# A written-out order of issue gets a list of its own for its beginning: first-layer weights first, first group in pieces

## The chip, the core and the metric

The kernel runs on one core of one Trainium2 chip. Its engines are TensorE (PE; its weight loads are listed as PEld), VectorE (DVE), ScalarE (ACT), GpSimd (POOL) and SyncE (SP), which here only issues DMAs. Each engine works through its own instructions in program order, and waits for another engine or for a DMA at a semaphore. The metric is the device time of one execution in microseconds; three runs of the kernel before gave 1090.84, 1091.98 and 1093.44, with a median of 1091.98.

## The reference

There are 128 graphs of 128 nodes with 64 features, and two layers, each followed by a residual sum and a layer norm. The first layer has a hidden width of 192; the second is a gated recurrent update.

```python
mask = (adj > 0.0)
xj_proj = x @ W1a                                  # W1 = [W1a; W1b]
diff = x[:, :, None, :] - x[:, None, :, :]
h = relu(xj_proj[:, :, None, :] + diff @ W1b + b1) # b, j, k, 192
hm = einsum('bjkh,bjk->bjh', h, mask)
x = layernorm(x + hm @ W2 + deg[..., None] * b2)
# second layer, on the new x
m = relu(relu(x @ V1 + c1) @ V2 + c2)
msg = relu(adj @ m)
gi, gh = msg @ W_ih.T + b_ih, x @ W_hh.T + b_hh    # three gates of 64 each
r, z = sigmoid(i_r + h_r), sigmoid(i_z + h_z)
n = tanh(i_n + r * h_n)
x = layernorm(x + (1 - z) * n + z * x)
```

The sum over a node's neighbours in `hm` is nearly all of the work.

## The kernel before

**Tiling.** The 128 graphs go in 32 groups of four (`G = 4`). For a group the kernel loads the adjacency `adjT` (256 KB), `xT` (two transfers of 64 KB) and `x` (128 KB) in `load`. POOL makes the mask (`masks`, L390). A matmul and a DVE multiply give each neighbour its rank (`ranks`, `pc` and `rankT`), others the degrees (`degrees`, `pd`, `deg` and `larger`); from these come the overflow segments (`counts`, `offsets` with `past` and `own`, `places`). The DVE compares ranks with constants to make one-hot selections (`pick0` in eight steps, `pick1` in four, L498). The projections of the nodes are `values` (`pu`, two fp32 products and two of a bias in bf16, L508 and L511; ACT copies them to `uv`, L515), and `pieces` splits them into three bf16 parts (`b0`, `b1`, `b2`), with ACT, DVE, ACT and POOL taking turns; for the first group this goes graph by graph.

**The main work of a group** is 24 rounds, six for each of its four graphs. In a round ACT copies a row into a PSUM tile of two banks (`seed`, L561), PE adds the selected neighbours to it with twelve matmuls (`gather`, L592), and the DVE sums absolute values over it (`reduce`, L608). There are three such PSUM tiles, so at most three rounds are in flight. Of a graph's six rounds, four take `pick0` and are seeded from `uv`; two take `pick1` and are seeded from `us`, which is made in `over` (`pz`, L572). `owners` turns `own` (`pq`, `ownT`). Two more PSUM tiles of one bank, `ps_w`, serve all other products in turn: the product that is two further down the order waits until the tile has been read. The sums are put together on POOL (`together`), `second` ends the first layer, and `message1` to `update` are the second layer.

**What sets the order.** A planner does not run on the chip; the order is written out. Every part is a generator that stops at its `yield`s. `TIMETABLE` gives for each part the due time of each of its steps in a group; a group's times are shifted by `PER = 768` per group. All steps of all groups are sorted by due time and emitted in that order, and the instructions of a step are queued on their engines in that order. The times have no other meaning. For group 0 the list `FIRST` replaces the times of the parts that it names, and `SETUP` gives the times of the five steps of `setup`, which makes the constants and loads the weights.

**The beginning as it is emitted.** First come the transfers of group 0, then all of `setup`'s first block: SP issues two transfers of the first layer's weights (`wab`), `w2c`, `b1c`, and five rows that are spread over all 128 partitions (`b2bc`, `bias` from `b1`, `bi` from `b_ih`, `bias` from `b_hh` and from `g_b2`; L148). The first layer's folded weights (`wall`, `wT`, `cps`, `dps`) follow, and then one block that folds the bias rows and splits all 576 columns of `bias` into three bf16 rows in `three` (L202 to L219, eight DVE operations). The first 256 columns of `three` serve the first layer's `values`; the other 320 serve `message2` and `gates`. Then group 0's `values`, `pieces`, `pick0`, `offsets` and `places` come. A last step of `setup`, at -3000, clears `gw1` and `gw2` on the DVE (L223) and issues twelve transfers of the second layer's weights (L225 to L231). Only behind these comes the load of group 1 (at 768 - 1520 = -752), then `masks` of group 1 (-3), the load of group 2 (16), `degrees` and `ranks` of group 1 (208 to 315), `over` and `owners` of group 0 and, from 476 on, group 0's rounds: `seed`, `gather`, `reduce`.

Of the kernel before, what the change touches and what calls it, by code (L numbers as in the profile page):

```python
# [8 lines left out]
F32 = mybir.dt.float32  # L9
# [3 lines left out]
ALU = mybir.AluOpType  # L13
AX = mybir.AxisListType

N = 128
F = 64
H = 192
HC = 96
G = 4  # L20
K = 64
V = H + F
W0 = 8
W1 = 4
# [23 lines left out]
}  # L48


SETUP = (-4990, -4988, -4987, -4981, -3000)
FIRST = {
    "load": (-5000,), "masks": (-4989,), "ranks": (-4986, -4985), "degrees": (-4984, -4983), "counts": (-4982,),
    "offsets": (-4980, -4979, -4966, -4965, -4964, -4963, -4962), "turned": (-4978, -4977),
    "values0": (-4976, -4975, -4974), "values1": (-4971, -4970, -4969), "pieces": (-4972, -4968, -4959, -4958),
    "places": (-4961, -4960), "pick0": (-4973, -4973, -4967, -4967, -4957, -4957, -4956, -4956),
}


# [18 lines left out]
def adj_resnorm_kernel(  # L78
# [19 lines left out]
    nc = tc.nc  # L98
    NB = x.shape[1]
    ng = NB // G  # L100
    const = ctx.enter_context(tc.tile_pool(name="const", bufs=1))


    ident = const.tile([N, N], F32, name="ident")
    ident_h = const.tile([N, N], BF16, name="ident_h")
    upper = const.tile([N, N], F32, name="upper")
# [3 lines left out]
    strict = const.tile([N, N], BF16, name="strict")  # L110
    strict_w = const.tile([N, N], BF16, name="strict_w")
# [3 lines left out]
    zeros = const.tile([N, 512], BF16, name="zeros")  # L115
    nhalf = const.tile([N, G], F32, name="nhalf")
    nseg_all = const.tile([N, NB], BF16, name="nseg_all")
    iota = const.tile([N, N], BF16, name="iota")

    wab = const.tile([N, 2, H], F32, name="wab")  # L120
    wall = const.tile([N, 4 * N], F32, name="wall")
    w2c = const.tile([HC, 2, F], F32, name="w2c")
    b1c = const.tile([HC, 2], F32, name="b1c")
    b2bc = const.tile([N, F], F32, name="b2bc")
# [3 lines left out]
    NBI = V + 256 + F  # L128
    bias = const.tile([N, NBI], F32, name="bias")
    three = const.tile([N, NBI], BF16, name="three")  # L130
    bi = const.tile([N, H], F32, name="bi")
# [10 lines left out]
    def each(t, n):  # L142

        return t.rearrange("p (o c) -> p o c", o=1).to_broadcast([t.shape[0], n, t.shape[1]])

    def setup(ps_g, ps_w):
        def spread(t, src):
            nc.sync.dma_start(t, src.rearrange("(o n) -> o n", o=1).to_broadcast(list(t.shape)))  # L148

        for h in range(2):  # L150
            nc.sync.dma_start(wab[h * F : (h + 1) * F], w1.rearrange("(c f) h -> f c h", c=2))
        nc.sync.dma_start(w2c, w2.rearrange("(c h) f -> h c f", c=2))
        nc.sync.dma_start(b1c, b1.rearrange("(c h) -> h c", c=2))
        spread(b2bc, b2)
        spread(bias[:, 0:H], b1)
        spread(bi, b_ih)
        spread(bias[:, V + F : V + 256], b_hh)
        spread(bias[:, V + 256 : NBI], g_b2)
        make_identity(nc, ident)
        make_upper_triangular(nc, upper)  # L160
        nc.gpsimd.memset(nhalf, -0.5)
        nc.vector.memset(ones_h, 1.0)
        nc.vector.memset(halves, 0.0)
        for h in range(2):
            nc.vector.memset(halves[h * K : (h + 1) * K, h : h + 1], 1.0)
        nc.vector.memset(zeros, 0.0)
        nc.vector.tensor_copy(incl2, upper)
        nc.vector.memset(incl2[0:K, K:N], 0.0)
        nc.vector.tensor_copy(ident_h, ident)
        nc.vector.tensor_copy(incl, upper)  # L170
        nc.vector.tensor_sub(strict, upper, ident)
        nc.vector.tensor_scalar_mul(strict_w, strict, -float(W1))

        for i in range(3):
            p = ps_g.tile([N, 2, 512], F32, tag="g", name="pv")
            for c in range(2):
                nc.tensor.matmul(p[:, c, :], ones_h, zeros, start=True, stop=True)
        ips = ps_w.tile([N, N], F32, tag="w", name="ips")
        nc.tensor.matmul(ips, ones_h, strict, start=True, stop=True)
        yield  # L180
        nc.vector.tensor_copy(iota, ips)
        nc.vector.tensor_add(wall[:, 0:H], wab[:, 0, :], wab[:, 1, :])
        nc.vector.tensor_scalar_mul(wall[:, V : V + H], wab[:, 1, :], -1.0)
        nc.vector.tensor_scalar_mul(w2c, w2c, 0.5)
        yield

        tps = ps_w.tile([HC, 4, F], F32, tag="w", name="tps")
        for c in range(4):
            at = (V, V + HC, 0, HC)[c]
            nc.tensor.transpose(tps[:, c, :], wall[0:F, at : at + HC], ident[0:F, 0:F])  # L190
        nc.vector.tensor_copy(wT, tps.rearrange("p c (o f) -> p c o f", o=1).to_broadcast([HC, 4, 2, F]))
        yield
        cps = ps_w.tile([N, F], F32, tag="w", name="cps")
        for c in range(2):
            nc.tensor.matmul(cps, b1c[:, c : c + 1].to_broadcast([HC, N]), w2c[:, c, :], start=c == 0, stop=c == 1)
        dps = ps_w.tile([N, 2, F], F32, tag="w", name="dps")
        for d in range(2):
            for c in range(2):
                nc.tensor.matmul(dps[:, d, :], wT[:, 2 * d + c], w2c[:, c, :], start=c == 0, stop=c == 1)
        nc.vector.tensor_copy(wall[:, H:V], dps[:, 0, :])  # L200
        nc.vector.tensor_copy(wall[:, V + H : 4 * N], dps[:, 1, :])
        nc.vector.tensor_add(bias[:, H:V], cps, b2bc)  # L202
        nc.vector.tensor_copy(bias[:, V : V + F], bi[:, 128:H])
        nc.vector.tensor_add(bias[:, V + F : V + H], bias[:, V + F : V + H], bi[:, 0:128])

        nc.vector.tensor_scalar_mul(bias[:, V + 256 : NBI], bias[:, V + 256 : NBI], 0.5)
        at = const.tile([N, 3], F32, name="at")
        nc.vector.tensor_add(at, ident[:, 0:3], ident[:, F : F + 3])
        piece = const.tile([N, NBI], BF16, name="piece")
        for c in range(3):  # L210
            nc.vector.tensor_copy(piece, bias)
            if c == 0:
                nc.vector.tensor_scalar(three, piece, at[:, c : c + 1], None, ALU.mult)
            else:
                nc.vector.scalar_tensor_tensor(
                    out=three, in0=piece, scalar=at[:, c : c + 1], in1=three, op0=ALU.mult, op1=ALU.add
                )
            if c < 2:
                nc.vector.tensor_sub(bias, bias, piece)  # L219
        yield  # L220

        for t, src in ((gw1, g_w1), (gw2, g_w2)):
            nc.vector.memset(t, 0.0)  # L223
            for h in range(2):
                nc.sync.dma_start(t[h * F : (h + 1) * F, h * F : (h + 1) * F], src)  # L225
        for h in range(2):
            hs = slice(h * F, (h + 1) * F)
            nc.sync.dma_start(gb1[hs], g_b1.rearrange("(h o) -> h o", o=1))
            nc.sync.dma_start(wm[hs, 0:F], w_ihT[:, 128:H])
            nc.sync.dma_start(wm[hs, F:H], w_ihT[:, 0:128])  # L230
            nc.sync.dma_start(wx[hs, :], w_hhT)  # L231

    def wide(t, n, w=F):
        return t.rearrange("p (g o) -> p g o", o=1).to_broadcast([N, n, w])
# [130 lines left out]
    with ExitStack() as fast:  # L365
# [4 lines left out]
        ps_g = fast.enter_context(tc.tile_pool(name="ps_g", bufs=3, space=bass.MemoryType.PSUM))  # L370
        ps_w = fast.enter_context(tc.tile_pool(name="ps_w", bufs=2, space=bass.MemoryType.PSUM))

        def load(s):
            g = s["g"]
            gs = slice(g * G, (g + 1) * G)
            s["adjT"] = loads.tile([N, G, N], F32, tag="adjT", name=f"adjT{g}")
            nc.sync.dma_start(s["adjT"], adjT[:, gs, :])

            s["xT"] = loads.tile([N, 2, N], F32, tag="xT", name=f"xT{g}")
            for h in range(2):  # L380
                nc.sync.dma_start(s["xT"][h * F : (h + 1) * F], xT[:, g * G + 2 * h : g * G + 2 * h + 2, :])
            s["x"] = loads.tile([N, G, F], F32, tag="x", name=f"x{g}")
            nc.sync.dma_start(s["x"], x[:, gs, :])

        def prep_parts(s):
            g = s["g"]
# [287 lines left out]
        def storer(g):  # L674
            return lambda o: nc.sync.dma_start(out[:, g * G : (g + 1) * G, :], o)

        def loading(s):
            def part():
                load(s)
                yield  # L680

            return part

        plan = {}
        name, g, run = "setup", -1, setup(ps_g, ps_w)
        for t in SETUP:
# [1 line left out]
        for g in range(ng):  # L688
            s = states[g]
            parts = {"load": loading(s), **prep_parts(s), **tail_parts(s, work, ps_w, G, storer(g))}  # L690
            parts.update({"seed": seeds(s), "gather": gathers(s), "reduce": reduces(s)})
            for i in range(G):
                parts.update({f"base{i}": base(s, i), f"together{i}": together(s, i)})
            for i in (0, 2):
                parts.update({f"over{i}": over(s, i), f"sums{i}": sums(s, i)})
            for name, times in TIMETABLE.items():
                run = parts[name]()
                for t in FIRST.get(name, times) if g == 0 else times:
                    plan.setdefault(g * PER + t, []).append(run)
        with tc.manual_schedule():  # L700
            for t in sorted(plan):
# [125 lines left out]
```

## Time and profile before

| | before |
|---|---|
| three runs, median | 1091.98 us (1090.84 to 1093.44) |
| the profiled execution | 1093.45 us, of which its span is 1091.4 |
| DVE, PE, ACT, POOL busy | 91, 87, 86, 77% of the span |
| mean granted TensorE clock | 0.983 |
| first `gather` matmul starts | 49.44 us |
| first `reduce` starts | 50.70 us |
| load of group 1 issued | 40.40 us |

The profile is of one execution. A line of the timeline has the start in microseconds, the busy time, the engine, the line of the code, the operation with what it writes and reads, how many such instructions are merged, and in brackets how long the engine sat idle before it and what released it. "SPq" is the DMA queue of SP. A group line of the page has the number of instructions, their busy time and the mean of one in nanoseconds. A line of the table of stretches gives, for each engine, its busy time and the number of its instructions in that stretch, then the granted TensorE clock, the mean share of the 16 DMA engines and the rate in GB/s.

### The profile page before, as it was taken

How to read it: one execution, taken by the hardware profiler on the slowest of the kernel's cores; microseconds unless marked ns; L12 is line 12 of the kernel's file. 1: busy time of each engine (PE TensorE's matmuls, PEld its weight loads, DVE VectorE, ACT ScalarE, POOL GpSimd, SP SyncE). 2: the span in 40 equal slices, each digit the busy share in tenths (PEclk: the TensorE clock that was granted, in tenths of full speed). 3: DMA queues.
4: the chain of work that ended last, by engine and by line, in shares of the span. 5: the costliest groups of instructions: out<-in, count | busy, mean ns of one | idle time of the engine just before them, and what ended most of it. 6: DMA issues, size and time to landing. Idle time of an engine off the chain costs nothing.

```text
span 1091.4 us, 33569 instructions
## 1 busy us (share of the span) xinstructions
PE 953.2 (87%) x13432; PEld 777.2 (71%) x13432; DVE 989.6 (91%) x2343; ACT 934.3 (86%) x1576; POOL 840.2 (77%) x1227
## 2 busy tenths in 40 slices
PE   5378999999999999999999999999999999999882
PEld 2267777777777777777777777777777777777661
DVE  4399999999999999999999999999999999999961
ACT  2399999999999999999999999999999999999850
POOL 1255688888888888888888888888888888888756
PEclk9999999999999999999999999999999999999985
DMA  1200000000000000000000000000000000000000
GB/s 41 68 2 22 21 22 5 24 25 22 26 26 26 26 7 25 22 26 26 26 26 9 24 21 26 26 26 26 24 8 26 21 26 26 26 7 7 7 6 21
DMA packets 21489, 24.04 MB, mean 22 GB/s; under 512 B 4049, under 2 KB 17233, under 8 KB 21329
## 3 DMA queue, kind: packets, MB, share of 16 engines
q1 hardware_dynamic: 21328, 21.85, 6.9%
q8 instruction: 107, 1.75, 0.7%
q14 instruction: 54, 0.43, 0.1%
HBM read 17.65 MB, written 4.19 MB: 20 GB/s over the span
## 4 chain that ended last, share of the span: by engine, by line
PE 36%; POOL 24%; DVE 18%; ACT 16%; issue 3%; SPq 1%; DMA 1%; POOLq 0%; DVEq 0%; ACTq 0%
PE pv L592 16%; DVE part L608 12%; ACT pv L561 10%; PE pu L508 4%; ACT b L527 3%; POOL part L634 2%; POOL rs L261 2%; POOL part L637 2%; POOL part L630 2%; DVE pick L498 2%; PE pm L291 2%; PE pw L273 2%; PE pa L309 2%; POOL uc L351 2%; POOL ub L348 1%
## 5 line engine op out<-in xcount | busy, mean ns | idle before, releaser
L608 DVE TENSOR_REDUCE part<-pv 128x192 f32<-128x768 f32 x768 | 709.2, 946 | 19.6 <-PE pv L592 13.9
L592 PE MATMUL pv<-b,pick 64*128 64x192 bf16 x9216 | 496.2, 244 | 63.4 <-ACT pv L561 62.1
L592 PEld LDWEIGHTS <-pick 64*128 64x128 bf16 x9216 | 385.0, 94 | 153.3 <-issue 124.2
L561 ACT COPY pv<-uv 128x768 f32<-128x768 f32 x512 | 409.4, 810 | 36.9 <-DVE part L608 33.1
L561 ACT COPY pv<-us 128x768 f32<-128x768 f32 x256 | 206.4, 806 | 17.7 <-DVE part L608 11.3
L630 POOL TENSOR_TENSOR part<-part 128x384 f32<-128x384 f32 x128 | 127.7, 997 | 79.7 <-DVE part L608 78.9
L515 ACT COPY uv<-pu 128x512 f32<-128x512 f32 x128 | 68.4, 586 | 29.1 <-PE pu L511 29.1
L650 PE MATMUL ph<-ownT,part 128*96 128x128 f32 x512 | 89.3, 276 | 1.0 <-POOL part L637 1.0
L536 POOL TENSOR_TENSOR b<-r,b 128x1024 bf16<-128x1024 f32 (+1 forms) x35 | 69.0, 1971 | 26.4 <-ACT b L533 26.4
L508 PE MATMUL pu<-wall,xT 64*128 64x512 f32 x256 | 86.4, 638 | 0.6 <-ACT uv L515 0.6
L498 DVE TENSOR_SCALAR pick<-rankT 128x512 bf16<-128x512 bf16 x256 | 83.4, 327 | 0.0
L634 POOL TENSOR_TENSOR part<-part 128x192 f32<-128x192 f32 x128 | 78.1, 610 | 2.5
L273 PE MATMUL pw<-w2c,hmT 96*128 96x64 f32 x512 | 79.2, 287 | 0.5 <-ACT hmT L656 0.5
L649 PE MATMUL ph<-ident,part 128*96 128x128 f32 x256 | 72.0, 281 | 6.9 <-ACT pv L561 6.8
L637 POOL TENSOR_TENSOR part<-part 128x192 f32<-128x192 f32 x128 | 77.1, 602 | 0.0
L448 POOL CAST own<-own 128x512 f32<-128x512 bf16 x32 | 19.5, 609 | 73.9 <-DVE own L442 73.9
L273 PEld LDWEIGHTS pw<-w2c,hmT 96*128 96x128 f32 x512 | 67.8, 193 | 10.6 <-ACT hmT L656 5.5
L632 POOL TENSOR_TENSOR part<-part 128x192 f32<-128x192 f32 x128 | 74.1, 589 | 0.0
L650 PEld LDWEIGHTS ph<-ownT,part 128*96 128x96 f32 x512 | 71.1, 167 | 2.7 <-POOL part L637 1.6
L261 POOL TENSOR_TENSOR rs<-ve,nhalf 128x4 f32<-128x4 f32 x64 | 66.5, 1039 | 5.3
L530 POOL TENSOR_TENSOR r<-uv,b 128x1024 f32<-128x1024 f32 x31 | 66.1, 2132 | 0.0
L572 PE MATMUL pz<-uv,own 128*128 128x192 f32 x256 | 60.0, 358 | 0.1
(136 smaller groups left out, 1625.7 us busy)
## 6 DMA issues: line engine op xcount, KB each, us to landing
adjT<-in_adjT_dram SPq DMA_DIRECT2D x32, 256.0 KB, 2.8
xT<-in_xT_dram SPq DMA_DIRECT2D x64, 64.0 KB, 2.8
x<-in_x_dram SPq DMA_DIRECT2D x32, 128.0 KB, 2.4
out_dram<-o SPq DMA_DIRECT2D x32, 128.0 KB, 1.7
wab<-in_w_dram SPq DMA_DIRECT2D x2, 96.0 KB, 2.7
bias<-in_b_dram SPq DMA_DIRECT2D x1, 96.0 KB, 6.1
bi<-in_b_ih_dram SPq DMA_DIRECT2D x1, 96.0 KB, 7.3
bias<-in_b_hh_dram SPq DMA_DIRECT2D x1, 96.0 KB, 7.1
```

Of the source, the lines that this page charges most:

```text
L261: nc.gpsimd.tensor_tensor(rs, ve, nhalf[:, 0:n], ALU.pow)
L273: nc.tensor.matmul(p[:, i, :], s["hmT"][:, i, c, :], w2c[:, c, :], start=c == 0, stop=False)
L498: nc.vector.tensor_scalar(s[name][:, i], s[src], float(first + i), None, ALU.is_equal)
L508: nc.tensor.matmul(ps[h], s["xT"][ks, i, :], wall[ks, :], start=True, stop=False)
L561: nc.scalar.copy(v, src.rearrange("p (c b h) -> p c b h", c=1, b=1).to_broadcast(list(v.shape)))
L592: nc.tensor.matmul(v[:, h, j, :], pick[ks, a + j, i, :], s[f"b{c}"][ks, i, F : F + H], start=False, stop=c == 2, skip_group_check=True,)
L608: nc.vector.tensor_reduce(into, view(s["pv", i, k]).rearrange("p c b h -> p h c b"), AX.XY, ALU.add, apply_absolute_value=True,)
L630: nc.gpsimd.tensor_tensor(f[:, 0:2], f[:, 0:2], f[:, 2:4], ALU.add)
L632: nc.gpsimd.tensor_tensor(f[:, 0], f[:, 0], f[:, 1], ALU.add)
L634: nc.gpsimd.tensor_tensor(f[:, 0], f[:, 0], f[:, no], ALU.subtract)
L637: nc.gpsimd.tensor_tensor(f[:, 0], f[:, 0], f[:, 1], ALU.add)
L650: nc.tensor.matmul(p[:, i, c, :], s["part1", i0 + i][:, 0, cs], s["ownT"][:, i0 + i, :], start=False, stop=True, skip_group_check=True,)
```

## The change

`FIRST` and `SETUP` get other times, `FIRST` also names `pick1`, `over0` and the first four steps of `seed`, `gather` and `reduce`; where `FIRST` names fewer steps than a part has, the rest keep their times of `TIMETABLE`. `setup` is cut into eight steps in place of five, and `load` of group 0 into two.

```diff
-SETUP = (-4990, -4988, -4987, -4981, -3000)
+SETUP = (-8001, -7999, -7610, -7530, -7400, -7380, -700, -690)
 FIRST = {
-    "load": (-5000,), "masks": (-4989,), "ranks": (-4986, -4985), "degrees": (-4984, -4983), "counts": (-4982,),
...
+    "load": (-8000, -7998), "masks": (-7580,), "ranks": (-7520, -7515), "degrees": (-7389, -7388), "counts": (-7387,),
+    "offsets": (-7372, -7371, -7366, -7366, -7366, -7366, -7365), "turned": (-7359, -7358),
+    "values0": (-7375, -7374, -7370), "values1": (-7368, -7364, -7360), "pieces": (-7373, -7363, -7355, -7350),
+    "places": (-7357, -7356), "pick0": (-7512, -7512, -7512, -7512, -7365, -7365, -7365, -7365),
+    "pick1": (-7352, -7352, -7351, -7351), "over0": (-7349, -7348), "seed": (-7369, -7366, -7361, -7354),
+    "gather": (-7367, -7362, -7354, -7351), "reduce": (-7365, -7358, -7353, -7350),
 }
...
+    def three_rows(cs, piece, at):
+        for c in range(3):
+            nc.vector.tensor_copy(piece[:, cs], bias[:, cs])
+            if c == 0:
+                nc.vector.tensor_scalar(three[:, cs], piece[:, cs], at[:, c : c + 1], None, ALU.mult)
+            else:
+                nc.vector.scalar_tensor_tensor(
+                    out=three[:, cs], in0=piece[:, cs], scalar=at[:, c : c + 1], in1=three[:, cs],
+                    op0=ALU.mult, op1=ALU.add,
+                )
+            if c < 2:
+                nc.vector.tensor_sub(bias[:, cs], bias[:, cs], piece[:, cs])
...
         for h in range(2):
             nc.sync.dma_start(wab[h * F : (h + 1) * F], w1.rearrange("(c f) h -> f c h", c=2))
+        yield
+        nc.vector.memset(bias, 0.0)
         nc.sync.dma_start(w2c, w2.rearrange("(c h) f -> h c f", c=2))
+        for h in range(2):
+            spread(bias[h * F : h * F + 3, 0:H], b1)
+            spread(bias[h * F : h * F + 3, H:V], b2)
         nc.sync.dma_start(b1c, b1.rearrange("(c h) -> h c", c=2))
-        spread(b2bc, b2)
-        spread(bias[:, 0:H], b1)
-        spread(bi, b_ih)
-        spread(bias[:, V + F : V + 256], b_hh)
-        spread(bias[:, V + 256 : NBI], g_b2)
...
-        nc.vector.tensor_add(bias[:, H:V], cps, b2bc)
-        nc.vector.tensor_copy(bias[:, V : V + F], bi[:, 128:H])
...
+        nc.vector.tensor_add(bias[:, H:V], bias[:, H:V], cps)
+        yield
         piece = const.tile([N, NBI], BF16, name="piece")
-        for c in range(3):
-            nc.vector.tensor_copy(piece, bias)
...
+        three_rows(slice(0, V), piece, at)
         yield
 
         for t, src in ((gw1, g_w1), (gw2, g_w2)):
             nc.vector.memset(t, 0.0)
             for h in range(2):
                 nc.sync.dma_start(t[h * F : (h + 1) * F, h * F : (h + 1) * F], src)
+        spread(bi, b_ih)
+        spread(bias[:, V + F : V + 256], b_hh)
+        spread(bias[:, V + 256 : NBI], g_b2)
+        spread(b2bc, b2)
         for h in range(2):
             hs = slice(h * F, (h + 1) * F)
             nc.sync.dma_start(gb1[hs], g_b1.rearrange("(h o) -> h o", o=1))
             nc.sync.dma_start(wm[hs, 0:F], w_ihT[:, 128:H])
             nc.sync.dma_start(wm[hs, F:H], w_ihT[:, 0:128])
             nc.sync.dma_start(wx[hs, :], w_hhT)
+        yield
+        nc.vector.tensor_copy(bias[:, V : V + F], bi[:, 128:H])
+        nc.vector.tensor_add(bias[:, V + F : V + H], bias[:, V + F : V + H], bi[:, 0:128])
+
+        nc.vector.tensor_scalar_mul(bias[:, V + 256 : NBI], bias[:, V + 256 : NBI], 0.5)
+        three_rows(slice(V, NBI), piece, at)
...
                 s["adjT"] = loads.tile([N, G, N], F32, tag="adjT", name=f"adjT{g}")
                 nc.sync.dma_start(s["adjT"], adjT[:, gs, :])
+                if g == 0:
+                    yield
...
             for name, times in TIMETABLE.items():
+                if g == 0 and name in FIRST:
+                    times = FIRST[name] + times[len(FIRST[name]) :]
                 run = parts[name]()
-                for t in FIRST.get(name, times) if g == 0 else times:
+                for t in times:
                     plan.setdefault(g * PER + t, []).append(run)
```

Inside the remaining steps some small operations trade places (the product `dps` goes ahead of `cps`, `at` is made with the constants). The order as it is then emitted: `wab`; `adjT` of group 0; the first layer's rows on three partitions, `w2c` and `b1c`; `xT` and `x` of group 0; the folding of the first layer's weights, with group 0's mask, ranks and four of its picks between; `three` for the first 256 columns (-7380); then group 0's `values`, `pieces`, `offsets` and four rounds of graph 0 in pieces between one another (-7375 to -7350), with `pick1` and the first `over`; the load of group 1 (-752); the clearing of `gw1` and `gw2` and all transfers of the second layer, now 16 (-700); the folding of its bias rows on the DVE (-690); and from there on the order of before, without the four rounds, `pick1` and the `over` that are already done.

More of the change, by code (lines that the diff above doesn't have):

```diff
@@ L48 @@
 }
-SETUP = (-4990, -4988, -4987, -4981, -3000)
+SETUP = (-8001, -7999, -7610, -7530, -7400, -7380, -700, -690)
 FIRST = {
-    "load": (-5000,), "masks": (-4989,), "ranks": (-4986, -4985), "degrees": (-4984, -4983), "counts": (-4982,),
-    "offsets": (-4980, -4979, -4966, -4965, -4964, -4963, -4962), "turned": (-4978, -4977),
-    "values0": (-4976, -4975, -4974), "values1": (-4971, -4970, -4969), "pieces": (-4972, -4968, -4959, -4958),
-    "places": (-4961, -4960), "pick0": (-4973, -4973, -4967, -4967, -4957, -4957, -4956, -4956),
+    "load": (-8000, -7998), "masks": (-7580,), "ranks": (-7520, -7515), "degrees": (-7389, -7388), "counts": (-7387,),
+    "offsets": (-7372, -7371, -7366, -7366, -7366, -7366, -7365), "turned": (-7359, -7358),
[3 rows of a table added]
+    "gather": (-7367, -7362, -7354, -7351), "reduce": (-7365, -7358, -7353, -7350),
 }
@@ L162, in setup @@
         nc.vector.memset(ones_h, 1.0)
+        nc.vector.memset(zeros, 0.0)
         nc.vector.memset(halves, 0.0)
@@ L165, in setup @@
             nc.vector.memset(halves[h * K : (h + 1) * K, h : h + 1], 1.0)
-        nc.vector.memset(zeros, 0.0)
+        nc.vector.tensor_copy(ident_h, ident)
+        nc.vector.tensor_sub(strict, upper, ident)
         nc.vector.tensor_copy(incl2, upper)
         nc.vector.memset(incl2[0:K, K:N], 0.0)
-        nc.vector.tensor_copy(ident_h, ident)
+        nc.vector.tensor_scalar_mul(strict_w, strict, -float(W1))
         nc.vector.tensor_copy(incl, upper)
-        nc.vector.tensor_sub(strict, upper, ident)
-        nc.vector.tensor_scalar_mul(strict_w, strict, -float(W1))
+        at = const.tile([N, 3], F32, name="at")
+        nc.vector.tensor_add(at, ident[:, 0:3], ident[:, F : F + 3])
         for i in range(3):
@@ L180, in setup @@
         yield
-        nc.vector.tensor_copy(iota, ips)
         nc.vector.tensor_add(wall[:, 0:H], wab[:, 0, :], wab[:, 1, :])
         nc.vector.tensor_scalar_mul(wall[:, V : V + H], wab[:, 1, :], -1.0)
+        nc.vector.tensor_copy(iota, ips)
         nc.vector.tensor_scalar_mul(w2c, w2c, 0.5)
@@ L188, in setup @@
         for c in range(4):
-            at = (V, V + HC, 0, HC)[c]
-            nc.tensor.transpose(tps[:, c, :], wall[0:F, at : at + HC], ident[0:F, 0:F])
+            cs = (V, V + HC, 0, HC)[c]
+            nc.tensor.transpose(tps[:, c, :], wall[0:F, cs : cs + HC], ident[0:F, 0:F])
         nc.vector.tensor_copy(wT, tps.rearrange("p c (o f) -> p c o f", o=1).to_broadcast([HC, 4, 2, F]))
         yield
-        cps = ps_w.tile([N, F], F32, tag="w", name="cps")
-        for c in range(2):
-            nc.tensor.matmul(cps, b1c[:, c : c + 1].to_broadcast([HC, N]), w2c[:, c, :], start=c == 0, stop=c == 1)
         dps = ps_w.tile([N, 2, F], F32, tag="w", name="dps")
@@ L199, in setup @@
                 nc.tensor.matmul(dps[:, d, :], wT[:, 2 * d + c], w2c[:, c, :], start=c == 0, stop=c == 1)
+        cps = ps_w.tile([N, F], F32, tag="w", name="cps")
+        for c in range(2):
+            nc.tensor.matmul(cps, b1c[:, c : c + 1].to_broadcast([HC, N]), w2c[:, c, :], start=c == 0, stop=c == 1)
         nc.vector.tensor_copy(wall[:, H:V], dps[:, 0, :])
         nc.vector.tensor_copy(wall[:, V + H : 4 * N], dps[:, 1, :])
-        nc.vector.tensor_add(bias[:, H:V], cps, b2bc)
-        nc.vector.tensor_copy(bias[:, V : V + F], bi[:, 128:H])
[L204 to L208, printed above, removed]
-        piece = const.tile([N, NBI], BF16, name="piece")
-        for c in range(3):
-            nc.vector.tensor_copy(piece, bias)
[L212 to L219, printed above, removed]
+        nc.vector.tensor_add(bias[:, H:V], bias[:, H:V], cps)
+        yield
+        piece = const.tile([N, NBI], BF16, name="piece")
+        three_rows(slice(0, V), piece, at)
         yield
@@ L371, in adj_resnorm_kernel, with loading, part @@
         ps_w = fast.enter_context(tc.tile_pool(name="ps_w", bufs=2, space=bass.MemoryType.PSUM))
[L373 to L383, printed above, removed]
+        def loading(s):
+            def part():
+                g = s["g"]
+                gs = slice(g * G, (g + 1) * G)
+                s["adjT"] = loads.tile([N, G, N], F32, tag="adjT", name=f"adjT{g}")
+                nc.sync.dma_start(s["adjT"], adjT[:, gs, :])
+                if g == 0:
+                    yield
+                s["xT"] = loads.tile([N, 2, N], F32, tag="xT", name=f"xT{g}")
+                for h in range(2):
+                    nc.sync.dma_start(s["xT"][h * F : (h + 1) * F], xT[:, g * G + 2 * h : g * G + 2 * h + 2, :])
+                s["x"] = loads.tile([N, G, F], F32, tag="x", name=f"x{g}")
+                nc.sync.dma_start(s["x"], x[:, gs, :])
+                yield
+            return part
         def prep_parts(s):
@@ L675, in storer @@
             return lambda o: nc.sync.dma_start(out[:, g * G : (g + 1) * G, :], o)
[L677 to L682, printed above, removed]
         plan = {}
```

## The prediction

> **What bounds the kernel now.** I read the page first, then the timeline of the first 65 us, the waits in it, the issues of DMAs and the chain that ended last. The page:
>
> ```profile
> span 1091.4 us, 33569 instructions
> ...
> PE 953.2 (87%) x13432; PEld 777.2 (71%) x13432; DVE 989.6 (91%) x2343; ACT 934.3 (86%) x1576; POOL 840.2 (77%) x1227
> ...
> L608 DVE TENSOR_REDUCE part<-pv 128x192 f32<-128x768 f32 x768 | 709.2, 946 | 19.6 <-PE pv L592 13.9
> ```
>
> The body is a loop of ACT, PE and DVE with the DVE nearly full; the change touches none of it after group 0. In the chain `L630` comes back at 204.81, 236.30 and 267.79: 31.49 us per group. So the change is worth what it moves the moment at which the rounds run full, and the rest follows rigidly. What stands before that moment, in order of time:
>
> ```profile
> 13.31 2.82 PE L508 MATMUL pu<-wall,xT 64*128 64x512 f32 x4
> 15.05 0.20 DVE L206 TENSOR_SCALAR bias<-bias 128x64 f32<-128x64 f32 x1 [0.63 <-DMA bias<-in_g_b_dram]
> 20.22 0.40 PE L511 MATMUL pu<-three,ones_h 64*128 64x256 bf16 x2 [4.10 <-DVE three L215]
> 32.63 0.31 DVE L223 MEMSET gw<- 128x128 f32 x2
> 32.83 2.41 SPq L225 DMA_DIRECT2D gw<-in_g_w_dram  x4
> 40.40 0.58 SPq L377 DMA_DIRECT2D adjT<-in_adjT_dram  x1
> 43.55 1.50 POOL L390 TENSOR_SCALAR maskT<-adjT 128x512 bf16<-128x512 f32 x1 [10.37 <-DMA adjT<-in_adjT_dram]
> 45.41 0.17 DVE L407 TENSOR_REDUCE deg<-pd 128x4 f32<-128x8 f32 x1 [12.15 <-PE pd L404]
> 49.44 2.80 PE L592 MATMUL pv<-b,pick 64*128 64x192 bf16 x36
> 56.91 4.72 DVE L608 TENSOR_REDUCE part<-pv 128x192 f32<-128x768 f32 x5
> ```
>
> The reader is to see two holes: PE waits at 16 to 20 us for `three`, which waits for rows the first layer doesn't need; and from 33 to 45 us every engine waits for group 1's adjacency, because its load stands on SP behind transfers that wait for a DVE clear at the end of group 0's preparation:
>
> ```profile
> SPq L225 <- DVE gw L223: 25.0, 1, 25.0
> ```
>
> My anchor is the end of the tenth `reduce` of group 0, the last of the five above: 56.91 + 4.72 = 61.63 us. From there on both orders hold the same work.
>
> **The change part by part.** I walk the new order with before's durations; a hand-over costs 0.02 to 0.1 us in the rows.
>
> *SP's first list.* An issue takes 0.4 to 0.65 us: `wab` from 0.73 to 2.03, `adjT` at 2.07, `w2c`, four small rows and `b1c` to 5.5, `xT` and `x` to 7.4, then group 1's load at once, at 7.4 in place of 40.40. With the landings shown (2.4 to 2.9) `wab` is there at 4.2, `adjT` at 4.95, `xT` at 8.8. The clear of `bias` (0.6, by the 0.27 of the 256-wide one) lies under `wab`'s flight; the small rows land near 6.7 (2.0, by `b1c`), and are read at 10.1.
>
> *To `three`.* `wall` is ready at 4.85, `tps` after the six warm-up products and `ips` 4.95 to 5.6, `wT` to 6.3; the mask 4.95 to 6.45 (1.50), `pc` to 7.1, `rankT` to 7.8, four picks 0.9 to 8.7. `dps` (1.92) and `cps` (1.12) follow `pc` on PE to 10.1, the `bias` sum to 10.35, degrees to 10.7. `three` is cut from 576 to 256 columns: 4.89 us (15.28 to 20.17) becomes about 2.4, to 13.1.
>
> *First values.* `pu` starts behind `pd` at 10.4 and takes the row's 2.82, to 13.2; `three` is just ready. So the 4.10 us wait on it goes; what is late next is fp32 `pu` itself. `uv` (0.58) and graph 0's pieces (0.42, 0.43, 0.40, 0.67) end at 16.25; `off` and the second `uv` on ACT to 16.2; first seed to 17.0; second `pu` (2.56, its tile is free at 16.25) to 18.9. The gather stands behind it on PE: 18.9 to 19.9 at the 0.93 for twelve that the first 36 took (2.80). First `reduce` at 19.95.
>
> *The rest of the first list, where DVE, ACT and PE take turns.* DVE: `reduce` to 20.9, `r` of graph 1 to 21.35, second `reduce` to 22.3. ACT: `b1` 21.8, seed 22.6, `uv` 23.15, `rank` 23.7. PE `ps` to 24.8, ACT `place` 25.4, `b0` 25.8, DVE `r` 26.3, third `reduce` 27.25, `pick1` 28.2, `r` 28.65, fourth `reduce` to 29.6. The four rounds cost the list some 4 us of DVE and as much ACT, mostly in gaps. So the clear of `gw1` comes at T = 29.6, against 32.63.
>
> *The new wait.* SP is held by that clear as before. From T + 0.2 it issues `gw` (2.45), then `bi` at T + 2.65 and, 0.47 apart, `b_hh` and `g_b2` (T + 3.6), then `b2bc` and eight more. The DVE's next instructions, straight behind the clear, are the copies from these three rows. Queued behind them on the DVE are `others`, `deg`, `larger` and `rankT` of group 1, picks and all further `reduce`; `over2`'s `pz` and `owners`' `pq` on PE wait for the PSUM tiles that `larger` and `rankT` must read; ACT waits for `pz`, so no further seed comes. All engines stand, as they stood for `adjT` before. With L from issue to landing of `g_b2`, the scaling (0.2) and 320 columns of `three` (4.89 scaled, 2.95), the DVE is free at T2 = T + 6.8 + L.
>
> ```profile
> b1c<-in_b_dram SPq DMA_DIRECT2D x1, 0.8 KB, 2.0
> b2bc<-in_b_dram SPq DMA_DIRECT2D x1, 32.0 KB, 4.7
> bias<-in_g_b_dram SPq DMA_DIRECT2D x1, 32.0 KB, 7.6
> ```
>
> L is not shown for this queue. Below, a lone small row took 2.0; above, `g_b2` took 7.6 behind four others. Between: five spreads, 352 KB, took from 5.53 (first issue) to 15.03, which less 2.0 is 21 ns per KB; the 256 KB of the four spreads now take 7.4 from T + 2.65, so L = 6.4; without `b2bc`, which is behind, 5.8. I take 5.9, nearer the upper row because the kind and order of transfer are that row's. T2 = 42.3.
>
> The DMA page of the Trainium skill ("DMA: Bandwidth & Descriptors", rules for kernel authors) speaks against this part: issue a transfer early, work, and wait late, so that its fixed cost overlaps. Its fixed cost of about 2 us alone would make T2 38.4 and the gain 9.1; the 7.6 row says that a spread takes far longer here.
>
> *From T2 to the anchor.* DVE: `others` 0.40, `deg` and `larger` 0.3, `rankT` 0.69. PE: `pz` 1.65 from T2 + 0.75, `pq` to T2 + 3.05. ACT: `us` 0.48, `ownT` 0.59, `base2` 0.46, seed five 0.81, to T2 + 4.9. Gather five to 5.85, group 1's `pu` (2.6 cold) to 8.5, gather six to 9.35, its `reduce` 9.4; five `reduce` of 0.95 end at T2 + 14.1. So the gain is 61.63 - 42.3 - 14.1 = 5.2 us.
>
> *What costs nothing.* `masks` of group 1 (1.50) and its products run under the wait; four rounds, `over` and `pick1` are gone from the stretch behind it; 16 issues and group 2's load (near 39, before 42.8) are ahead of their readers. If the wait were gone, the 16 issues (9.6 us) would delay nothing until group 2's mask.
>
> *Cold products.* The 2.82 for four `pu` is not the engine's usual pace:
>
> ```profile
> 12.50:16.20 3.70, 2.82 (x4) 1.00 (x4) 1.00 0.08 25
> 21.00:24.50 3.50, 2.56 (x4) 0.98 (x4) 1.00 0.00 0
> 53.80:55.20 1.40, 1.07 (x4) 0.32 (x4) 1.00 0.00 0
> ```
>
> The granted clock is 1.00 in all three stretches of that line, the duration 2.6 times as long in the early ones, with PE busy nearly without a gap from 9.4 to 16.1. "TensorE: Matmul & The Clock Gate" of the Trainium skill (the clock gate, part 1) has a pace doubled after some 3.4 us of steady work; by it both early `pu` would run at 1.07, and the gain be some 7.5. The row speaks for slow ones, and I keep 2.82 and 2.56. As an end of the range, both `pu` at 1.07 put T at about 27.3; some forty hand-overs 0.05 us longer put it at 31.6.
>
> **The sum.** 1093.45 of the profiled execution less 5.2 gives 1088.25; that execution was 1.47 above the median, and against the median 1091.98 the forecast is 1086.8. The gain is 47.5 - T - 6.8 - L: from 1.5 (T 31.6, L 7.6) to 11.4 (T 27.3, L 2.0).
>
> **Rivals.**
> A, the rows land quickly: they have no 0.7 MB of other loads in front, as they had at 5.5 us. L near 2 to 4 gives a gain of 7 to 9, some 1084. Against it: at 7 to 15 us, with those loads done, the DMA engines were 4 to 27% busy and the rows still crawled.
> B, no change: the first rounds are done early, but the second hole is as long as the first, since T comes late. Zero gain at T = 34.8. For it speaks that ACT, DVE and PE alternate with few instructions in flight; against it that all of before's preparation, with its 4.10 us hole, ended at 32.6. 1092.
> C, slower: spreads are slowed by what is issued behind them. Before, nothing followed `g_b2`; now 0.2 MB of `wm`, `wx` and `b2bc` and then 0.5 MB of group 2 do. Place: the DVE's first copy behind the clear. With 0.2 MB at 21 ns per KB, L is 10 and the gain 1; it turns to a loss over 0.2% at L above 13.3. If group 2's 512 KB shared the pace too, L would be some 17 and the time 1098. Against it: the five rows landed in the order of their issue, with the earliest the quickest (4.7 to 7.6).
> D, it doesn't do what it says would need the small rows to be late at 10.1 us; they have 3.4 us to spare.
>
> **How the numbers follow.** Forecast 0.64, A 0.13, B 0.10, C 0.13. What can be told from no change is 0.2%, 2.2 us. The forecast's own range, T 28.5 to 31.6 and L 4.7 to 7.6, is a gain of 7.5 to 1.5 (1084.5 to 1090.5); a small part of it, 0.03, lies within 0.2%. With A's 1083 below and the near part of B above, the range is 1083.0 to 1091.5. Faster 0.74 (0.61 and A), same 0.13, slower 0.13.
>
> **What would show it.** `adjT` of group 1 issued near 7.4; no DVE wait of 4 us at `three`; first `reduce` near 20 and four before 30; clear of `gw1` near 29.6; then a DVE wait of some 9 us on `bi` and `g_b2`, with PE and ACT idle; the tenth `reduce` ending near 56.4; 31.49 us per group after it. I am wrong if that wait is much shorter or longer, if T is off, or if the pace per group changes: 0.17 us per group over 31 groups would cancel the gain.

## The result, and the profile after

The changed kernel took 1084.41 us (median of 5, 1083.6 to 1086.64) beside 1091.09 us of the kernel before (median of 5, 1090.66 to 1093.44). The ratio is 0.9938 with a 95% interval of 0.9921 to 0.9956: 6.7 us faster. The forecast was 1086.8, with a gain of 5.2. In the 31 later runs of the kernel before, beside the experiments, its median was 1092.18; against that the gain would be 7.8.

From the page of the changed kernel:

```profile
span 1081.8 us, 33583 instructions
...
PE 952.1 (88%) x13432; PEld 778.3 (72%) x13432; DVE 992.6 (92%) x2352; ACT 934.4 (86%) x1576; POOL 840.4 (78%) x1227
...
L628 DVE TENSOR_REDUCE part<-pv 128x192 f32<-128x768 f32 x768 | 709.2, 946 | 21.8 <-PE pv L612 14.9
```

The work is the same, to the 0.1 us of `reduce`. What moved is the beginning. Its timeline, in order of time (the columns are those of the timeline of before):

```profile
6.82 0.43 SPq L392 DMA_DIRECT2D adjT<-in_adjT_dram  x1
10.27 2.23 PE L528 MATMUL pu<-wall,xT 64*128 64x512 f32 x4 [0.23 <-DVE bias L220]
13.30 0.40 PE L531 MATMUL pu<-three,ones_h 64*128 64x256 bf16 x2 [0.80 <-DVE three L155]
19.61 0.94 DVE L628 TENSOR_REDUCE part<-pv 128x192 f32<-128x768 f32 x1
28.33 0.31 DVE L227 MEMSET gw<- 128x128 f32 x2
34.31 0.19 DVE L241 COPY bias<-bi 128x64 f32<-128x64 f32 x1 [5.68 <-DMA bi<-in_b_ih_dram]
36.02 0.20 DVE L244 TENSOR_SCALAR bias<-bias 128x64 f32<-128x64 f32 x1 [0.96 <-DMA bias<-in_g_b_dram]
39.06 0.55 DVE L155 SCALAR_TENSOR_TENSOR three<-piece,at,three 128x320 bf16<-128x320 bf16 x1
40.10 1.62 PE L592 MATMUL pz<-uv,own 128*128 128x192 f32 x4 [9.38 <-DVE larger L429]
44.78 1.99 PE L528 MATMUL pu<-wall,xT 64*128 64x512 f32 x4
45.13 0.96 DVE L628 TENSOR_REDUCE part<-pv 128x192 f32<-128x768 f32 x1 [3.78 <-PE pv L612]
47.99 4.72 DVE L628 TENSOR_REDUCE part<-pv 128x192 f32<-128x768 f32 x5
```

Group 1's load goes out at 6.82 in place of 40.40, the wait for `three` shrank from 4.10 to 0.80 us, and four rounds are done before 28.4. Then all engines stand again, for the second layer's bias rows: the DVE waits 5.68 us for `bi`, a little for `b_hh` and 0.96 us for `g_b2`, folds them until 39.5, and only then reads group 1's degrees, for which PE (9.38 us) and behind it ACT have stood. The tenth `reduce`, the anchor of the prediction, ends at 47.99 + 4.72 = 52.71 us, against 61.63: 8.9 us earlier. After it `L650` returns at 195.87, 227.36 and 258.85, still 31.49 us per group.

The two spans differ by 9.6 us, the medians of the runs by 6.7. A second profiled execution of each kernel, below, shows the tenth `reduce` at 61.83 and 52.02. So the shift at the beginning repeats; from the tenth `reduce` to the mask of the last group the same kernel took 910.6 and 912.2 us (before) or 911.2 and 912.2 (after), and the ending after it another 117.5 to 119.2. These 1 to 2 us come and go between executions. Both profiled executions of before (1093.45, 1093.59) were longer than most of its runs, which explains part of the 9.6; whether its runs without a profile begin earlier too can't be seen.

### The profile page after: what moved, and what is told of

The parts are those of the page before. It is cut to its first block, busy times and chain, and to the rows that moved or that the text cites. A ratio compares the mean times of both kernels' runs of the same rounds, so it can differ in the third digit from the quotient of the medians.

```text
span 1081.8 us, 33583 instructions
## 1 busy us (share of the span) xinstructions
PE 952.1 (88%) x13432; PEld 778.3 (72%) x13432; DVE 992.6 (92%) x2352; ACT 934.4 (86%) x1576; POOL 840.4 (78%) x1227
## 4 chain that ended last, share of the span: by engine, by line
PE 34%; POOL 25%; DVE 20%; ACT 16%; issue 3%; DMA 1%; SPq 0%; POOLq 0%; ACTq 0%; DVEq 0%
PE pv L612 16%; DVE part L628 13%; ACT pv L581 10%; PE pu L528 4%; POOL part L654 3%; POOL part L657 3%; ACT b L547 3%; POOL rs L275 2%; POOL part L650 2%; DVE pick L518 2%; PE pm L305 2%; PE pa L323 2%; POOL uc L365 2%; POOL ub L362 2%; POOL y L368 2%
## 5 line engine op out<-in xcount | busy, mean ns | idle before, releaser
L650 POOL TENSOR_TENSOR part<-part 128x384 f32<-128x384 f32 x128 | 127.8, 998 | 76.4 <-DVE part L628 76.2
```

Of the source, the lines that this page charges most:

```text
L650: nc.gpsimd.tensor_tensor(f[:, 0:2], f[:, 0:2], f[:, 2:4], ALU.add)
```

## The experiments

The theory, M: in the beginning one hole after another holds all engines; the tenth `reduce` moves with the last of them, and the rest of the time follows one for one (at 31.49 us per group). Rivals: R1, the four rounds done in pieces are the gain; R2, the split of `three` is. The table has the median of each run, that of the kernel before beside it, and the end of the tenth `reduce` in the profiled execution:

| run | edit | us | before | ratio (95%) | tenth `reduce` ends |
|---|---|---|---|---|---|
| the change | | 1084.41 | 1091.09 | 0.9938 (0.9921 to 0.9956) | 52.71 |
| e2_load_ahead | before, group 1's load ahead | 1084.19 | 1092.18 | 0.9920 (0.9904 to 0.9935) | 53.34 |
| e6_split_only | before, `three` split | 1088.05 | 1092.06 | 0.9964 (0.9950 to 0.9978) | 56.81 |
| e8_split_load | before, both | 1078.68 | 1092.06 | 0.9879 (0.9863 to 0.9894) | 47.33 |
| e3_load_behind | after, load behind again | 1088.43 | 1092.18 | 0.9963 (0.9949 to 0.9977) | 56.24 |
| e1_fold_late | after, folding in the body | 1082.61 | 1092.18 | 0.9919 (0.9902 to 0.9935) | 43.08 |
| e5_rows_early | after, bias rows loaded early | 1077.32 | 1092.06 | 0.9861 (0.9846 to 0.9876) | 46.51 |
| e7_fold_pieces | e5, folding in three pieces | 1076.44 | 1092.06 | 0.9851 (0.9836 to 0.9866) | 43.06 |
| e4_rounds_back | after, no early rounds | 1080.26 | 1092.18 | 0.9905 (0.9887 to 0.9922) | 49.61 |
| e9_early_norounds | e5, no early rounds | 1075.44 | 1092.58 | 0.9851 (0.9834 to 0.9867) | 44.25 |
| e10_fold_in_gap | e9, folding in an idle gap | 1074.31 | 1092.58 | 0.9832 (0.9815 to 0.9850) | 42.84 |
| after_again, before_again | unchanged, one profile each | 1084.27, 1093.59 | | | 52.02, 61.83 |

"One for one" holds within 1 us in seven of these runs: the shift of the tenth `reduce` from 61.63 and the gain of the median agree so far. In the change itself, in e3_load_behind and in e7_fold_pieces 1.6 to 3 us of the shift don't arrive, and in e1_fold_late 9 us, for a reason of its own.

### One part of the change alone, on the kernel before

```diff
-SETUP = (-4990, -4988, -4987, -4981, -3000)
+SETUP = (-4990, -4988, -4987, -4981, -700)
```

> The kernel before, with one number changed: the last step of setup (clear of gw1 and gw2, twelve transfers of the second layer) is due at -700 in place of -3000, so that group 1's load goes ahead of it. Theory M: the hole of before from 33 to 45 us goes, group 1's degrees start at about 34.9 in place of 45.1, the time falls by some 10 us to 1081, more than the whole change brought. Rival R1 (the change gained by its early rounds) and rival R2 (it gained by three being split, the 4.1 us hole at 16 us): the load alone brings 0 to 2 us, 1089 to 1091.

One number brought 8.0 us, as much as the whole change: the medians, 1084.19 and 1084.41, are the same within what the runs vary by. The tenth `reduce` came 8.3 us earlier, against 8.9. M holds against both rivals, but its size was too large by 2 us. The trace of this run:

```profile
33.82 0.31 DVE L223 MEMSET gw<- 128x128 f32 x2
34.34 1.50 POOL L390 TENSOR_SCALAR maskT<-adjT 128x512 bf16<-128x512 f32 x1
36.28 0.15 DVE L409 TENSOR_REDUCE larger<-pd 128x4 f32<-128x8 f32 x1
```

The clear, the end of the first group's preparation, came at 33.82 in place of 32.63, because the bias rows landed later: `bi` 7.9 us after its issue and `g_b2` 8.8, against 7.3 and 7.6 (7.5 and 7.9 in before_again). Group 1's load now goes out right behind them, but that this is the reason isn't shown: in e8_split_load, below, it does so too, and they landed after 7.4 and 7.9. And the mask of group 1, in order on POOL behind group 0's last piece, is what decides next.

The split of `three` alone:

```diff
...
+        three_rows(slice(0, V), piece, at)
...
             nc.sync.dma_start(wx[hs, :], w_hhT)
+        nc.vector.tensor_copy(bias[:, V : V + F], bi[:, 128:H])
+        nc.vector.tensor_add(bias[:, V + F : V + H], bias[:, V + F : V + H], bi[:, 0:128])
+        nc.vector.tensor_scalar_mul(bias[:, V + 256 : NBI], bias[:, V + 256 : NBI], 0.5)
+        three_rows(slice(V, NBI), piece, at)
```

> The kernel before, with the folding split alone: the first 256 columns of three where they were, the other 320 (and the rows they need) behind the second layer's transfers, where the DVE stood for group 1's adjacency anyway. Theory M: three is ready before pu (16.1 us), so the 4.1 us hole on PE goes, the clear of gw1 and with it group 1's load come 4 us earlier, the time is 1086 to 1088. Rival R2 (this split is the gain of the change): 1084. If the take-turns of ACT, DVE and POOL decide there: 1090 to 1091.

4.0 us, with the clear at 28.19 in place of 32.63. As M has it; R2 falls, since the split alone is not the gain of the change.

> The kernel before with two small edits together and no round in pieces: the split of the folding (e6_split_only) and group 1's load ahead of the second layer's transfers (e2_load_ahead). Theory M: 10.2 and 4.1 us add, less some 2 us because the 3.5 us of folding now stands in front of group 0's rounds with no hole over it: 1078 to 1080, faster than the changed kernel without its first list. Rival R1 (the rounds in pieces are needed): no faster than 1084.

The two small edits together, with no list of its own and no round in pieces, gave 1078.68: as expected, and 5.7 us under the changed kernel. So R1 falls too, and something in the rest of the change costs time.

### The new hole

```diff
-SETUP = (-8001, -7999, -7610, -7530, -7400, -7380, -700, -690)
+SETUP = (-8001, -7999, -7610, -7530, -7400, -7380, -700, 1450)
```

> The changed kernel, with only the folding of the second layer's bias rows on the DVE taken from behind the clear of gw1 (due time -690) to 1450, in the loaded body ahead of its first reader. Theory M (the anchor moves with the new hole on the DVE, from the clear at 28.3 us to 39.5 us, and everything behind shifts rigidly): the DVE goes on at 28.7, the mask of group 1 (ready at 29.95) decides next, the tenth reduce of group 0 ends near 43.5 in place of 52.7, and the time falls by 9 less up to 3.5 us of folding that now lies in a nearly full DVE: 1075 to 1079. Rival R1 (the hole hides behind something else, the gain is that of the four early rounds): no change, 1083 to 1086.

The tenth `reduce` ended at 43.08, as M has it (43.5), 9.6 us earlier than in the changed kernel. But the time fell by 1.8 only (1082.61). The loss has a place: two successive masks on POOL, of groups 3 and 4, came 40.0 us apart (70.82 and 110.81), where in the changed kernel they are 32.7 us apart. The folding stands there:

```profile
69.61 0.73 DVE L151 CAST piece<-bias 128x320 bf16<-128x320 f32 x1
70.82 1.51 POOL L410 TENSOR_SCALAR maskT<-adjT 128x512 bf16<-128x512 f32 x1
72.29 1.06 POOL L650 TENSOR_TENSOR part<-part 128x384 f32<-128x384 f32 x1
72.54 1.16 DVE L155 SCALAR_TENSOR_TENSOR three<-piece,at,three 128x320 bf16<-128x320 bf16 x1
```

From the scaling on it took 5.7 us (69.39 to 75.05) and not 3.5: the cast 0.73 in place of 0.33, the product 1.16 in place of 0.55, beside POOL. And as it lay in one piece, the three PSUM tiles were full and ACT waited 5.98 us. So 3.5 us of DVE work in a hole became 7 us of time in the full body.

Taking the wait away and leaving the work:

```diff
+    def second_layer():      # gw1, gw2 cleared; the 16 transfers
...
+        plan.setdefault(-7950, []).append(second_layer())
...
+                if g == 1 and name == "load":
+                    times = (-7960 - PER,)
```

> The changed kernel, with group 1's load and then all 16 transfers of the second layer issued right behind group 0's loads (gw1 and gw2 are cleared among the first constants); the folding of the bias rows stays where it is, behind the last early round. It tells the waiting from the work in the new hole. Theory M: the wait for the rows (5.7, 0.3 and 1.0 us) and for SP goes, the folding of 3.5 us stays: the DVE is free near 32.0 in place of 39.5, the tenth reduce ends near 45.2, the time is 1076 to 1078. If the hole were the folding itself: within 1 us of the changed kernel. If the early spreads slow the loads of group 0 in front of them, the first reduce comes later than 19.6.

1077.32, the first `reduce` at 19.72: the early transfers delay it by 0.1 us (the fourth by 0.5), and the tenth `reduce` is 6.2 us earlier than in the changed kernel. The folding (28.75 to 33.3) waits for nothing now. So of the hole of 11.2 us (28.33 to 39.53) the waits, 6.9 us, were worth 6.2 us at the tenth `reduce` and 7.1 in the medians, and the folding is the rest.

> As e5_rows_early, with the folding of the second layer's bias rows cut into three pieces that lie where the DVE stood idle: one between the second and third early reduce (2.9 us idle there in the changed kernel), two in front of the fifth reduce (3.8 us idle there). Theory M: another 1.5 to 2.5 us off e5_rows_early, as group 1's mask and degrees (30.3 us) decide next: tenth reduce near 43.5, time 1074 to 1076. If the DVE is not what decides there any more: the time of e5_rows_early.

The tenth `reduce` came at 43.06, 3.45 us before e5_rows_early, and the last group's mask still 3.4 us earlier (954.77 against 958.17), but the medians differ by 0.9 only, and 1076.44 is just above the expected 1074 to 1076. The ending of this profiled execution was 120.8 us long, against 118.2, and from 1000 to 1040 us the granted clock was 0.91 in it, against 0.96. M holds at the beginning; how much of it reaches the time here isn't shown.

### Group 1's load put back

```diff
+                if g == 1 and name == "load":
+                    times = (-695 - PER,)
```

> The changed kernel, with group 1's load put back behind the 16 transfers of the second layer. Theory M: adjT of group 1 is issued near 38.1 us, its degrees start near 42.8 in place of being ready at 30.3, which is 3.3 us behind the DVE hole that now decides; the tenth reduce ends near 56 and the time is 1087 to 1088. A theory by which the load's place is the whole gain: back to 1091.

1088.43, the tenth `reduce` 3.5 us later, group 1's `larger` at 43.51. The early load is worth only 4 us inside the change, where it was worth 8.0 alone: behind it stood the other hole.

### The four rounds in pieces

```diff
     "places": (-7357, -7356), "pick0": (-7512, -7512, -7512, -7512, -7365, -7365, -7365, -7365),
-    "pick1": (-7352, -7352, -7351, -7351), "over0": (-7349, -7348), "seed": (-7369, -7366, -7361, -7354),
-    "gather": (-7367, -7362, -7354, -7351), "reduce": (-7365, -7358, -7353, -7350),
+    "pick1": (-7352, -7352, -7351, -7351), "over0": (-7349, -7348),
```

> The changed kernel, with the first four seeds, gathers and reduces of group 0 at their old due times (the rest of the first list as changed). Theory M: the clear of gw1 comes some 2.8 us earlier (25.5), the hole is as long and ends near 36.7, and four rounds of 1.0 to 1.2 us come behind it: the tenth reduce near 54.3, the time 1085 to 1087, 1 to 2 us slower than the changed kernel. Rival R1 (the rounds in pieces carry the gain): 1089 to 1091.

The expectation had the sign wrong: without the early rounds the kernel is 4 us faster (1080.26), the tenth `reduce` 3.1 us earlier. The timeline of this run:

```profile
24.81 0.31 DVE L226 MEMSET gw<- 128x128 f32 x2
32.25 0.19 DVE L243 TENSOR_SCALAR bias<-bias 128x64 f32<-128x64 f32 x1 [0.82 <-DMA bias<-in_g_b_dram]
36.33 1.62 PE L591 MATMUL pz<-uv,own 128*128 128x192 f32 x4 [8.07 <-DVE larger L428]
39.56 1.82 DVE L627 TENSOR_REDUCE part<-pv 128x192 f32<-128x768 f32 x2 [2.39 <-PE pv L611]
42.76 1.07 PE L527 MATMUL pu<-wall,xT 64*128 64x512 f32 x4
44.90 4.71 DVE L627 TENSOR_REDUCE part<-pv 128x192 f32<-128x768 f32 x5
```

In front of the hole the four rounds cost 3.5 us: the clear comes at 24.81 in place of 28.33, and the hole is as long (10.95 us to 35.76). Behind it they cost 0.7: from the end of the folding to the tenth `reduce` it takes 13.85 us with ten rounds and took 13.18 with six. There the DVE stood idle for 3.78 us anyway, until ACT and PE had worked through `pz`, `us`, `ownT` and the fifth seed; here it sums the four early rounds in that time, for they need none of that work. The rounds were taken out of a place where they were nearly free and put into a chain where each of their steps holds the next.

The idle DVE is not the whole reason for the 0.7. With the four rounds in front of them, group 1's four `pu` took 1.07 us here and not 1.99: the granted clock rose from 0.50 to 1.00 between 39 and 40 us, while in the changed kernel it was still 0.50 from 44 to 48. All eight profiled executions with these rounds behind show 1.06 or 1.07, all six with them in front 1.99. So the low price may owe some 0.9 us to the pace of the products that follow; no run separates the two.

The same step without the wait for the rows:

> As e5_rows_early (group 1's load and the second layer's transfers early, the folding at its place), but with the four rounds back at their old due times. It tells whether what e4_rounds_back showed (the rounds in pieces cost time, since behind the hole they would fill idle time of the DVE) depends on the wait for the rows. Theory M2 (they cost about 3 us because they delay everything behind them on ACT and DVE by 3.5 us, and the four rounds behind the hole cost only 0.7 us): the folding ends near 28.9 in place of 33.3, the tenth reduce near 42.8, the time 1073 to 1075, 3 us under e5_rows_early. If the rounds are harmful only together with the wait for the rows: the time of e5_rows_early, 1077.

1075.44, and 2.3 us earlier at the tenth `reduce` (44.25): the rounds cost there too, somewhat less. It stayed short of the 42.8 and of 1073 to 1075 expected. The folding ended at 30.2 and not 28.9, since three of its operations, beside POOL, took 0.59, 0.90 and 0.69 us in place of 0.30, 0.48 and 0.33.

> As e9_early_norounds, with the whole folding of the second layer's bias rows at -7356, where the DVE of e4_rounds_back stood idle for 3.4 us (19.4 to 22.8) while ACT turned places. Theory M2: group 1's degrees (27.6 us) decide next, the tenth reduce ends near 41.8, 1 us before e9_early_norounds: 1072 to 1074. If the DVE does not decide there: the time of e9_early_norounds.

The lowest median: 1074.31, 1.7% under the kernel before and 10 us under the changed one. The 1.1 us to e9_early_norounds are within what the runs of both vary by; at the tenth `reduce` it is 1.4. The folding lies in the gap, and group 1's degrees decide, behind the mask on POOL:

```profile
19.94 0.18 DVE L225 COPY bias<-bi 128x64 f32<-128x64 f32 x1
29.08 0.17 DVE L431 TENSOR_REDUCE deg<-pd 128x4 f32<-128x8 f32 x1 [2.81 <-PE pd L428]
```

The degrees come 1.5 us later than expected, and the tenth `reduce` 1.0, because graph 2's piece on the DVE (`r`, at 24.03) now waits for the folding (19.94 to 24.0) and POOL's last piece and the mask with it.

### Once more, unchanged

> The changed kernel once more, unchanged, for a second profiled execution: does the wait for the rows of the second layer (5.7, 0.3 and 1.0 us) and the end of the tenth reduce (52.7 us) repeat? If the landing is a property of the order, within 0.5 us; if of chance, the wait lies anywhere between 5 and 11 us.

> The kernel before once more, unchanged, for a second profiled execution: the tenth reduce should end within 1 us of 61.6, and what its span differs by from 1091.4 should lie behind the last group's mask (972.2 us), where the granted clock falls.

The waits for the rows were 5.57, 0.44 and 0.70 us, the tenth `reduce` 52.02; of the kernel before, 61.83. Both repeat within 0.7 us. The wait for `bi` was 5.85 and 5.49 us in e3_load_behind and e4_rounds_back, which issue these rows in the same order, so in four executions it went with the order. The span of before repeated too (1091.5), but not as expected: the last mask came 1.8 us later and the ending was 1.7 us shorter, so executions differ ahead of that mask as well.

## Why the prediction was right

The direction, the range and the mechanism held: no work is saved, the first hole of 4.10 us goes, group 1's load goes out at 6.82 (7.4 predicted), a new wait on the DVE for the bias rows takes the place of the one for `adjT`, all behind it stands, and the rest of the kernel follows rigidly at 31.49 us per group. But by its own signs the wait (some 9 us forecast, 6.9 measured) and the end of the tenth `reduce` (56.4 forecast, 52.71 measured) were off: there the gain was 8.9 and not 5.2. And 1084.41 lies just below the forecast's own 1084.5 to 1090.5, within the stated range only because that reaches down to A's 1083. By the steps of the working:

- *To `three`*: 13.24 us, predicted 13.1, by two errors that cancel: it began at 10.28 and not 10.7, and took 2.96 us and not 2.4. *First values*: the four `pu` took 2.23 and not 2.82, so `three` was last after all, by 0.80 us; neither the row's pace nor the 1.07 at the end of the range was met. First `reduce` 19.61 (19.95).
- *The first list*: T was 28.33 (29.6). 1.3 us too late.
- *The new wait*: from T to the issue of `g_b2` 3.72 us (3.6). L was 4.0 and not 5.9: this term of the sum was missized most, by 1.9 us. The pace of 21 ns per KB, worked out from the queue of before, didn't hold; `bi`, `b_hh` and `g_b2` were read 3.4, 3.2 and 4.0 us after their issue, against 7.3, 7.1 and 7.6. That is the condition of rival A, at its upper edge, and A's 1084 is the number that came. What makes the queue of before slower wasn't separated: other loads in front, or five spreads in place of four.
- *The folding* took 3.5 us with the scaling, not 3.15: 0.35 too little. The eight operations on `three` take 4.89 us for 576 columns, 3.36 for 320 and 2.96 for 256, so they shrink by less than scaling had it. T2 was 39.53 (42.3).
- *From T2 to the anchor* 13.2 us (14.1): `pu` took 1.99 in place of 2.6.

Together 1.3 - 0.1 + 1.9 - 0.35 + 0.9 = 3.65 us, the difference between 5.2 and 8.9. That 6.7 arrived in the medians, nearer the forecast, is thus luck and no merit of the sum.

One sentence was wrong, though the total didn't show it: that the four rounds lie "mostly in gaps" of the first list and are gone from the stretch behind. They cost 3.5 us in front and saved 0.7 behind (e4_rounds_back). The prediction walked through them, but never priced the list without them.

The rule of "DMA: Bandwidth & Descriptors" in the Trainium skill (rules for kernel authors) that spoke against the change, to issue early and wait late, is what e5_rows_early did, and it brought 7 us. Rival B (no change) would have needed T at 34.8, C (slower) L above 13.3; nothing slowed the spreads so. Whether transfers further behind slowed is open: `wm` landed after 4.0 to 4.4 us, against 2.0 to 2.2 before, but after 2.1 to 2.5 in e3_load_behind, which issues the same sixteen in the same order. D did not come: the small rows were read at 9.99 without a wait for a DMA.

## What to carry to other kernels

Before moving work forward into a chain of hand-overs, ask where it ran before: work that fills idle time behind a hole is nearly free there (0.7 us for four rounds), and each of its steps costs in the chain (3.5 us). On a queue that issues in order, look at what stands in front of the first transfer that the next stage needs; here one due time was worth 8 us, as much as the whole rewriting. And put the reader of a transfer well behind its issue, in a gap of its engine and not in the full body, where 3.5 us of DVE cost 7.

## What the runs showed of the hardware

- In these traces the granted clock of an early stretch can read 1.00 while the products run slow. The products of `pz` have a median of 527 ns in the kernel before at 45 to 49 us, with 1.00 in that column, and 528 ns in the kernel after at 40 to 42 us, with 0.50. The same products took 1.62 us for four there and 0.91 later. The durations tell the clock; the column didn't.
- Some DVE operations took about twice their time beside some of POOL's: in the folding of e1_fold_late 0.73 in place of 0.33, 0.90 in place of 0.48, 1.16 in place of 0.55 us, while POOL scaled rows, made a mask or added parts. In e7_fold_pieces one such product took 0.98 us during a mask and another 1.17 during an addition on POOL. "SBUF — State Buffer" of the Trainium skill (terms) has a pair of ports for which the two engines arbitrate, held for a whole instruction. The slow rows would fit that, but in e7_fold_pieces a difference of 0.48 us ran at its usual pace within the same mask (33.42, the mask from 32.54 to 34.03), and no run took POOL's work away: the cause is not shown.
